# A four-layer image network in one kernel on one Trainium2 core: new products in its linear attention, and softmax transfers made for two steps at a time

## The chip, the cores and the metric

One NeuronCore of a Trainium2 chip runs the whole program in one launch. The metric is the device time in microseconds (us) from the start of the program to its end. The engines have short names in the profile: PE is the matrix unit (PEld its weight loads), DVE the vector unit, ACT the scalar unit, POOL and SP the two others, which here mostly issue DMA transfers. "SPq L2173" means an issue on SP's queue by line 2173 of the kernel.

## What is computed

The input is x of shape 2 x 512 x 32 x 32 in float32; write HW = 1024 for the positions of an image. Four layers follow one another: layer 0 is a deformable cross attention with a learned bias and an MLP; layer 1 a deformable convolution with a gate; layer 2 a linear attention; layer 3 a group norm and an attention of eight heads of 64 channels. Only the last two matter here:

```
# layer 2, per image, C = 512 channels, N = 1024 positions, d = 64
Qf, Kf = delu(wq x + bq)^T, delu(wk x + bk)        # delu(z) = 10 relu(z) + exp(10 min(z, 0))
V      = wv x + bv
KV     = Kf V^T                                    # d x C
norm   = 1 / (Qf (sum over n of Kf + 1e-10))
x      = x + gamma * (Qf KV * norm)^T

# layer 3, per image, 8 heads of 64 channels
h       = group_norm(x)
q, k, v = split(W_qkv h + b_qkv)
attn    = softmax(q k / 8)                         # 1024 x 1024 per head
out     = x + W_out (attn v) + b_out
```

## The kernel before

Layers 0 and 1 take the first 2940 us and are not touched. From there the program is a set of Python generators that are woven together: each `yield` is a place where the caller lets another generator issue some instructions. PE runs its instructions in the order in which they are issued, and so do the other engines and the DMA queues; in layer 3 that order is the written one (`manual_schedule`).

**Layer 2** is `Linear.run` (lines 1761 to 1902), once for each image. It runs for image 0 beside the gathers of layer 1's deformable convolution for image 1, and for image 1 beside the first matrix products of layer 3 (`att.queries_keys` and `att.values` of image 0); the tuple `BESIDE` says how many yields of `values` go behind each yield of `linear.run`. Its parts in order: two matmul groups for queries and keys with `delu` on them (an addition of the bias, then four passes: DVE, ACT, DVE, DVE); eight rounds that transpose 128 positions of x (`px`) and copy them out (`xt2`); in rounds 1 and 2 the transposed keys `kf`, held twice side by side; in round 3 the key sums `pks` (line 1827), eight matmuls of `kf` with a matrix of ones; from round 3 on the products `pkx` (line 1794): for each of the eight position blocks, four matmuls that have a 128 x 128 block of `xt2` as the stationary operand and move 64 columns of keys; then `kx`, a copy of `pkx`, and the product with `wv`.

**Layer 3** first makes queries, keys and values of image 0, then runs `heads`: 64 steps of 128 query positions for a pair of heads each (`first` are 32 steps of image 0, `second` 32 of image 1). A step is:

- `logits` (line 2133): four matmuls into two banks of 128 x 1024, one for each head of the pair. There are two such banks in all, so the logits of the next step start when the exponentials of this one have read them.
- for each of the two banks, the maximum (DVE, line 2236), the exponential with its sum (ACT, line 2242), written into a room `e2` of 8 KB in each partition, then a reciprocal and a scaling (`divide`, line 2254).
- `turn`: DVE transposes each half in 32 x 32 blocks (line 2166); after the second half, 16 DMAs of 64 KB move the blocks to where the transpose of the whole matrix needs them (line 2173), alternately on SP's and on POOL's queue, from the room into the tile `aT`, which holds two steps. Two `aT` tiles exist.
- `weigh` (line 2183): 16 matmuls of `v` with two steps' `aT`, issued in two halves, four steps after the first of the two; the copy of its output (line 2193) overwrites the queries of that step.

`room(at)` gives a step its room. Steps with `at % 3 < 2` take the two buffers of the tile `e3`; each third step borrows 8 KB from what is free then: the last two blocks of `q1` (the queries of image 1, written later), the value weights `w_v`, or the values `v[0]` of image 0. A room's next writer waits until its transfers have landed. `LENT` holds the steps at which the place changes. `w_out` is loaded over `w_v` at the steps in `LOADED`, on ACT's queue.

Within a step the order on the engines is set by this part of the loop, which makes the logits and exponentials of step `at + 1` before it turns step `at`:

```
if g == 1:
    e2, ahead = ahead[0], weights(at + 1) if at + 1 < len(work) else ((), ())
    turn(at, e2, 0)
    for part in ahead[1][:1]:
        self.divide(*part)
    turn(at, e2, 1)
```

Between these, PE gets work from `fill`: (steps, generator, yields) in turn: the values of image 1, its queries and keys, and the output projections of image 0 and of the first half of image 1 (`project`; its matmuls, like those of the values, go through `by_columns`, line 1962, as two halves of 64 columns). One yield of them is one 128 x 128 stationary block against 512 columns. After the last step come what is left of the weighings and of the projections (`last`), and then the last projection, whose stores go out on SP's queue.

Of the kernel before, what the change touches and what calls it, by code (L numbers as in the profile page):

```python
# [11 lines left out]
F32 = mybir.dt.float32  # L12
# [265 lines left out]
def layers(net, out):  # L278
# [12 lines left out]
    with ExitStack() as later:  # L291
# [106 lines left out]
        with ExitStack() as l1:  # L398
# [95 lines left out]
            with ExitStack() as ctx:  # L494
# [6 lines left out]
                for i, _ in enumerate(linear.run(1, bank, held)):  # L501
                    some(keys, 2)
                    some(values, BESIDE[i])
                    if i > 11:
                        next(terms)
# [19 lines left out]
BESIDE = (1, 2, 1, 1, 1, 1, 1, 1, 1, 1, 3, 3, 1, 1, 1, 1)  # L525
# [1213 lines left out]
def delu(nc, out, e, z):  # L1739

    nc.vector.tensor_scalar(e, z, 0.0, None, ALU.min)
    nc.scalar.activation(e, e, AF.Exp, scale=10.0)
    nc.vector.tensor_scalar(out, z, 0.0, 10.0, ALU.max, ALU.mult)
    nc.vector.tensor_tensor(out, out, e, ALU.add)


class Linear:
# [5 lines left out]
    def __init__(self, net, ctx, **kw):  # L1753
# [4 lines left out]
        self.ones = w.tile([128, 64], F32, name="ones2", tag="ones2")  # L1758
        nc.gpsimd.memset(self.ones, 1.0)
# [4 lines left out]
    def run(self, b, bank, kv_bank):  # L1764
# [5 lines left out]
        qk = []  # L1770
        for n in range(2):
# [11 lines left out]
            nc.vector.tensor_scalar(qf, pqk, net.vec("bqk", n), None, ALU.add)  # L1783
            delu(nc, qf, e, qf)
# [5 lines left out]
        kf = tmp.tile([128, 8, 2, 64], F32, name="kf", tag="kf")  # L1790

        def product(t, xt):
            for cc in range(CC):
                nc.tensor.matmul(
                    pkx[:, 64 * cc : 64 * cc + 64],
                    lhsT=xt[:, 128 * cc : 128 * cc + 128],
                    rhs=kf[:, t, 0, :],
                    start=(t == 0 and cc == 0),
                    stop=(t == 7 and cc == CC - 1),
                    skip_group_check=True,  # L1800
                )

        for t in range(8):
# [5 lines left out]
            xt = tmp.tile([128, C], F32, name="xt2", tag="xt2", bufs=4)  # L1809
# [4 lines left out]
            if t in (1, 2):  # L1814
                n = t - 1
                pk = bank("pk")
                for u in range(4):
                    at = slice(128 * u, 128 * u + 128)
                    nc.tensor.transpose(pk[:, at], qk[n][:, at], ident)
                keys = pk.rearrange("p (t v d) -> p t v d", v=2, d=64)[:, :, 1 - n : 2 - n, :]  # L1820
                nc.scalar.copy(
                    kf[:, 4 * n : 4 * n + 4, :, :], keys.to_broadcast([128, 4, 2, 64])
                )
            if t == 3:
                pks = bank("pks")
                for u in range(8):
                    nc.tensor.matmul(
                        pks[:, :64],
                        lhsT=kf[:, u, :, :].rearrange("p v d -> p (v d)"),
                        rhs=self.ones,  # L1830
                        start=(u == 0),
                        stop=(u == 7),
                    )
                ksum, norms = (
                    tmp.tile([128, 64], F32, name=name, tag=name) for name in ("ksum", "norms")
                )
                nc.vector.tensor_copy(ksum, pks[:, :64])
                nc.vector.tensor_scalar(norms, ksum, 1e-10, None, ALU.add)
# [22 lines left out]
            if t > 2:  # L1861
# [5 lines left out]
        for part in pending:  # L1867
            product(*part)
        kx = tmp.tile([128, CC, 2, 64], F32, name="kx", tag="kx")
        nc.scalar.copy(  # L1870
            kx,
            pkx[:, : 64 * CC]
            .rearrange("p (c d) -> p c d", d=64)
            .unsqueeze(2)
            .to_broadcast([128, CC, 2, 64]),
        )
        yield
# [77 lines left out]
LENT = 27, 37  # L1955
LOADED = 38, 39, 40, 41
# [14 lines left out]
class Attention:  # L1971
# [20 lines left out]
    def open_values(self, ctx, **kw):  # L1992
# [4 lines left out]
        self.q1 = self.late.tile([128, CC, HW], F32, name="qk1", tag="qk1")  # L1997
        self.small = net.pool(ctx, "l3_small", 2, **kw)
        self.w_v = self.load_qkv(self.w_pool, 2)
        self.b_v = net.load_row("b_v_row", self.w_pool)  # L2000

    def load_out(self, k):

        if k == 0:
            self.w_out = self.w_pool.tile([128, CC, C], F32, name="w_out_t", tag="w_qkv2")
# [319 lines left out]
```

## Time and profile before

| what | value |
|---|---|
| times of three runs | 3664.64, 3664.69, 3670.85 us; median 3664.69 |
| the profiled execution | 3666.18 us; its span from first to last instruction 3664.2 us |
| granted PE clock, mean | 0.995 of full |
| PE busy in the span | 98% |
| 2940 to 3030 us (layer 2 of image 0 beside gathers) | PE busy 90.0 of 90.0 us, DVE 55.2, ACT 26.2 |
| 3178 to 3246 (layer 2 of image 1) | PE 68.0 of 68.0, DVE 27.2, ACT 9.6 |
| 3250.4 to 3631 (the 64 steps of layer 3) | PE 369.2 of 380.6, DVE 312.0, ACT 309.1, POOL 242.5; DMA share 0.66, 181 GB/s |
| 3631 to 3664.2 (after the last step) | PE 28.0 of 33.2 |

The profiled execution is one more run of the same program with the hardware's recorder on; all lines quoted below are from it. Rows of the windows view give the window, its length, then busy us and count for PE, PEld, DVE, ACT and POOL, then the granted PE clock, the mean busy share of the 16 DMA engines and their GB/s. Rows of the timeline give the start, the duration (of the whole group, where "x8" stands behind it), the engine, the line and the operation, and in brackets the idle time before it and what ended it; "SPq" rows are the issues of that queue. Rows of the waits view give who waited for what: us in total, times, longest. Rows of the chain, followed back from the last instruction, read like the timeline. A float32 matmul is two records of PE.

### The profile page before, as it was taken

To read this page: it belongs to the slowest core of one execution; us is meant where nothing else is said; L and a number is where in the kernel's file an instruction comes from. 1 tells how busy PE (TensorE), PEld (TensorE's weight loads), DVE (VectorE), ACT (ScalarE), POOL (GpSimd) and SP (SyncE) were. 2 spreads that over 40 slices of the span, in tenths; PEclk is the share of its full clock that TensorE was granted. 3 is DMA by queue.
4 is the path that set the end of the run, shared out by engine and by line. 5 is a ranking of instruction groups with operands and counts; after the bars stand their busy time and mean duration, and the time that the engine had idled before them with its cause. 6 is when DMAs were issued, how large, how long until landed. Compare 5 with 4: busy or idle time off the path is not lost.

```text
span 3664.2 us, 60466 instructions
## 1 busy us (share of the span) xinstructions
PE 3604.2 (98%) x24684; PEld 1402.5 (38%) x24684; DVE 2768.8 (76%) x3192; ACT 2591.6 (71%) x2885; POOL 417.3 (11%) x693
## 2 busy tenths in 40 slices
PE   7999999999999999999999999999999999999999
PEld 4333333333333333333333444444444454444444
DVE  6999999999999999999999821051048657268786
ACT  6999999999999999999999821131113324348875
POOL 0000000000000000000000000000025125026665
PEclk9999999999999999999999999999999999999999
DMA  3000000000000000000001010002246547126675
GB/s 117 1 24 24 17 9 24 24 1 24 24 24 1 24 24 24 1 24 24 1 24 58 16 49 0 0 26 79 70 137 227 179 162 274 37 70 184 174 197 171
DMA packets 96071, 235.80 MB, mean 64 GB/s; under 512 B 21252, under 2 KB 26884, under 8 KB 93108
## 3 DMA queue, kind: packets, MB, share of 16 engines
q0 software_dynamic: 38080, 112.47, 10.0%
q1 hardware_dynamic: 55844, 115.26, 9.7%
q10 hardware_dynamic: 1872, 4.22, 0.4%
q8 instruction: 195, 3.19, 0.4%
q14 instruction: 80, 0.66, 0.1%
HBM read 156.11 MB, written 8.65 MB: 45 GB/s over the span
## 4 chain that ended last, share of the span: by engine, by line
PE 73%; ACT 15%; DVE 5%; issue 3%; DMA 3%; POOL 1%; SPq 0%; DVEq 0%; ACTq 0%; POOLq 0%
PE ph L925 33%; PE ph L1186 6%; PE acc L1175 6%; ACT h L915 5%; PE sim L944 5%; PE po L1680 4%; ACT hi L1014 4%; ACT lo L1011 4%; PE pw L1544 3%; PE pl L2133 2%; PE po L2183 2%; PE pq L1968 2%; PE po L1126 2%; PE pq L1962 1%; DMA got<-table,idx 1%
## 5 line engine op out<-in xcount | busy, mean ns | idle before, releaser
L925 PE MATMUL ph<-h,w_t 128*32 128x512 f32 x16384 | 1796.8, 593 | 7.1 <-ACT h L915 3.9
L900 DVE TENSOR_TENSOR h<-ab 128x1024 f32<-128x1024 f32 x1024 | 1205.3, 1218 | 45.9 <-PE ph L925 44.0
L925 PEld LDWEIGHTS ph<-h,w_t 128*32 128x32 f32 x16384 | 565.2, 110 | 1203.5 <-issue 1067.0
L915 ACT ACTIVATE h<-h 128x1024 f32<-128x1024 f32 x832 | 925.2, 1112 | 8.6 <-DVE size L874 7.8
L937 DVE SCALAR_TENSOR_TENSOR hi<-lo,low_w,hi 128x1024 f32<-128x1024 f32 x512 | 654.3, 1278 | 20.1 <-ACT hi L1014 19.8
L1014 ACT ACTIVATE hi<-ph,size_b,size 128x1024 f32<-128x1024 f32 x512 | 644.1, 1258 | 21.6 <-PE ph L925 21.6
L1011 ACT ACTIVATE lo<-ph,vec_t 128x1024 f32<-128x1024 f32 x512 | 595.4, 1163 | 44.0 <-PE ph L925 39.0
L1680 PE MATMUL po<-fold,turned 128*128 128x512 f32 x576 | 261.7, 597 | 0.4 <-issue 0.4
L1194 ACT ACTIVATE h<-ph,vec_t 128x512 f32<-128x512 f32 x64 | 44.0, 687 | 303.1 <-PE ph L1186 303.0
L944 PE MATMUL sim<-hi,w 128*32 128x512 f32 x2048 | 249.4, 592 | 0.0
L1262 POOL MEMSET pad<- 128x136 f32 x2 | 0.4, 220 | 2061.1 <-PE ph L925 2061.1
L1186 PE MATMUL ph<-xn,room 128*128 128x512 f32 x512 | 230.8, 594 | 0.0
L1175 PE MATMUL acc<-h,mlp_w_t 128*128 128x512 f32 x512 | 229.8, 592 | 0.0
L1589 POOL DMA_INDIRECT got<-table,idx x144 | 156.7, 1088 | 538.2 <-DVE sum L1613 273.9
L1613 DVE SCALAR_TENSOR_TENSOR sum<-got,wts,sum 128x256 f32<-128x256 f32 x432 | 182.3, 478 | 40.3 <-ACT sum L1609 32.5
L2236 DVE TENSOR_REDUCE m<-pl 128x1 f32<-128x1024 f32 x128 | 150.7, 1219 | 61.1 <-PE pl L2133 60.5
L2173 POOL DMA_DIRECT2D aT<-e x344 | 168.2, 497 | 199.8 <-DVE s L2253 111.8
L1680 PEld LDWEIGHTS po<-fold,turned 128*128 128x128 f32 x576 | 105.0, 192 | 107.0 <-issue 106.4
L1642 ACT COPY turned<-pt 128x512 f32<-128x512 f32 x72 | 41.9, 582 | 146.9 <-PE pt L1636 136.4
L1175 PEld LDWEIGHTS acc<-h,mlp_w_t 128*128 128x128 f32 x512 | 97.3, 190 | 122.4 <-issue 121.7
L1186 PEld LDWEIGHTS ph<-xn,room 128*128 128x128 f32 x512 | 96.6, 191 | 117.0 <-issue 116.4
L1611 DVE TENSOR_SCALAR sum<-got,wts 128x256 f32<-128x256 f32 x38 | 12.4, 352 | 165.9 <-PE pt L1636 152.1
(274 smaller groups left out, 2980.5 us busy)
## 6 DMA issues: line engine op xcount, KB each, us to landing
ab<-feat_d SPq DMA_DIRECT2D x64, 512.0 KB, 4.6
aT<-e SPq DMA_DIRECT2D x344, 64.0 KB, 2.6
aT<-e POOLq DMA_DIRECT2D x344, 64.0 KB
room<-in_dc_w_dram SPq DMA_DIRECT2D x9, 1024.0 KB, 4.8
dc_w_t<-in_dc_w_dram SPq DMA_DIRECT2D x10, 512.0 KB, 4.1
aT<-qk SPq DMA_DIRECT2D x72, 64.0 KB, 2.7
aT<-qk POOLq DMA_DIRECT2D x72, 64.0 KB
aT<-v SPq DMA_DIRECT2D x72, 64.0 KB, 2.7
```

The source lines that it names most:

```text
L900: nc.vector.tensor_tensor(h1.rearrange("p (y x) -> p y x", x=32), at_x[:, k : k + 1, :].to_broadcast([128, 32, 32]), at_y[:, k, :].unsquee ...
L915: nc.scalar.activation(h1, h1, AF.Relu)
L925: nc.tensor.matmul(ph[32 * t : 32 * t + 32, half(n)], lhsT=w2[:, c0 : c0 + 32], rhs=pair[t // 2][:, half(n)], start=True, stop=True, skip_ ...
L937: nc.vector.scalar_tensor_tensor(hi, lo, low_w, hi, ALU.mult, ALU.add)
L944: nc.tensor.matmul(sim[32 * t : 32 * t + 32, half(n)], lhsT=w3[:, 30 - j : 62 - j], rhs=sums[t][:, half(n)], start=(j == 0), stop=(j == 30 ...
L1011: nc.scalar.activation(lo, phs[0], AF.Relu, bias=b2_lo)
L1014: nc.scalar.activation(hi, phs[1], AF.Relu, bias=size_b, scale=size)
L1175: nc.tensor.matmul(accs[oc], lhsT=self.w2[:, m, 128 * oc : 128 * oc + 128], rhs=hs[m], start=(m == 0), stop=(m == 15),)
L1186: nc.tensor.matmul(ph, lhsT=self.w1[:, k, 128 * m : 128 * m + 128], rhs=xn[:, k, :], start=(k == 0), stop=(k == CC - 1),)
L1613: nc.vector.scalar_tensor_tensor(t[:, q, :], g[:, s, :], w, t[:, q, :], ALU.mult, ALU.add)
L1680: nc.tensor.matmul(self.out, lhsT=turned[:, at : at + 128], rhs=self.folded.w[k][:, i, :], start=(k == 0 and i == 0), stop=(k == 8 and i = ...
L2173: (nc.sync, nc.gpsimd)[i % 2].dma_start(out=turned[at // 2][32 * u : 32 * u + 32, at % 2, a, :, :], in_=e2[32 * a : 32 * a + 32, u, :, :],)
```

## The change

In layer 2, `delu` takes its argument already multiplied by ten (the multiplication joins the addition of the bias) and so has one pass less; its last pass also gives the totals over positions. The key sums become one matmul of two columns of totals with a matrix that adds the two halves (`fold`). The products hold the keys stationary (64 columns) and move 512 columns of `xt2`; even and odd position blocks go to the two halves of the output's partitions, so a copy to `parts`, four transposes and two DVE passes follow, which put the result into the old layout of `kx`. One more yield stands in between, and `BESIDE` has one more entry.

In layer 3, `PAIRS` names for each pair of steps the place of its exponentials: `a` a tile of 16 KB in each partition, `q` and `w` parts of one new tile `shared` that holds `q1` (four blocks) and `w_v` (two blocks), `v` the values of image 0. A pair's transfers are issued together after its odd step: 16 DMAs of 128 KB, each for both steps, where there were 32 of 64 KB. The four pairs with a dot (steps 28 to 35) have single rooms and single transfers as before, by `SINGLE`. `w_out` is loaded one step earlier. Four yields of the values of image 1 (`lead`) go between the first exponentials and their scaling, and `fill` is shifted to match. After the last step, what is left of the projections goes ahead of the two last weighings, where it stood between them.

```diff
--- before
+++ after
@@ -503,3 +503,3 @@
                     some(values, BESIDE[i])
-                    if i > 11:
+                    if i > 12:
                         next(terms)
@@ -524,3 +524,3 @@
-BESIDE = (1, 2, 1, 1, 1, 1, 1, 1, 1, 1, 3, 3, 1, 1, 1, 1)
+BESIDE = (1, 2, 1, 1, 1, 1, 1, 1, 1, 1, 2, 2, 2, 1, 1, 1, 1)
@@ -1738,8 +1738,7 @@
-def delu(nc, out, e, z):
+def delu(nc, out, e, z, total):
     nc.vector.tensor_scalar(e, z, 0.0, None, ALU.min)
-    nc.scalar.activation(e, e, AF.Exp, scale=10.0)
-    nc.vector.tensor_scalar(out, z, 0.0, 10.0, ALU.max, ALU.mult)
-    nc.vector.tensor_tensor(out, out, e, ALU.add)
+    nc.scalar.activation(e, e, AF.Exp)
+    nc.vector.scalar_tensor_tensor(out, z, 0.0, e, ALU.max, ALU.add, accum_out=total)
@@ -1757,4 +1756,6 @@
         self.bv = net.load_row("bv_row", w)
-        self.ones = w.tile([128, 64], F32, name="ones2", tag="ones2")
-        nc.gpsimd.memset(self.ones, 1.0)
+        self.fold = w.tile([128, 2, 64], F32, name="halves", tag="halves")
+        ident = net.cst("ident")
+        for v in range(2):
+            nc.vector.tensor_tensor(self.fold[:, v, :], ident[:, :64], ident[:, 64:], ALU.add)
@@ -1770,2 +1771,3 @@
         qk = []
+        totals = tmp.tile([128, 4], F32, name="totals", tag="totals")
         for n in range(2):
@@ -1782,4 +1784,8 @@
             e = tmp.tile([128, 512], F32, name="e2", tag="e2")
-            nc.vector.tensor_scalar(qf, pqk, net.vec("bqk", n), None, ALU.add)
-            delu(nc, qf, e, qf)
+            nc.vector.tensor_scalar(qf, pqk, net.vec("bqk", n), 10.0, ALU.add, ALU.mult)
+            delu(nc, qf, e, qf, totals[:, n : n + 1])
+            rows = slice(64 * (1 - n), 128 - 64 * n)
+            nc.vector.tensor_copy(
+                totals[rows, 2:4], totals[rows, n : n + 1].to_broadcast([64, 2])
+            )
             qk.append(qf)
@@ -1789,14 +1795,14 @@
-        kf = tmp.tile([128, 8, 2, 64], F32, name="kf", tag="kf")
+        kf = tmp.tile([128, 8, 64], F32, name="kf", tag="kf")
         def product(t, xt):
-            for cc in range(CC):
-                nc.tensor.matmul(
-                    pkx[:, 64 * cc : 64 * cc + 64],
-                    lhsT=xt[:, 128 * cc : 128 * cc + 128],
-                    rhs=kf[:, t, 0, :],
-                    start=(t == 0 and cc == 0),
-                    stop=(t == 7 and cc == CC - 1),
-                    skip_group_check=True,
-                )
+            r = 64 * (t % 2)
+            nc.tensor.matmul(
+                pkx[r : r + 64, :],
+                lhsT=kf[:, t, :],
+                rhs=xt,
+                start=(t < 2),
+                stop=(t > 5),
+                skip_group_check=True,
+            )
@@ -1808,3 +1814,3 @@
                 )
-            xt = tmp.tile([128, C], F32, name="xt2", tag="xt2", bufs=4)
+            xt = tmp.tile([128, C], F32, name="xt2", tag="xt2", bufs=5)
             if t % 2 == 0:
@@ -1819,21 +1825,19 @@
                     nc.tensor.transpose(pk[:, at], qk[n][:, at], ident)
-                keys = pk.rearrange("p (t v d) -> p t v d", v=2, d=64)[:, :, 1 - n : 2 - n, :]
-                nc.scalar.copy(
-                    kf[:, 4 * n : 4 * n + 4, :, :], keys.to_broadcast([128, 4, 2, 64])
-                )
+                keys = pk.rearrange("p (t v d) -> p t v d", v=2, d=64)[:, :, 1 - n, :]
+                nc.scalar.copy(kf[:, 4 * n : 4 * n + 4, :], keys)
             if t == 3:
                 pks = bank("pks")
-                for u in range(8):
-                    nc.tensor.matmul(
-                        pks[:, :64],
-                        lhsT=kf[:, u, :, :].rearrange("p v d -> p (v d)"),
-                        rhs=self.ones,
-                        start=(u == 0),
-                        stop=(u == 7),
-                    )
-                ksum, norms = (
-                    tmp.tile([128, 64], F32, name=name, tag=name) for name in ("ksum", "norms")
+                nc.tensor.matmul(
+                    pks[:, :2],
+                    lhsT=self.fold.rearrange("p v d -> p (v d)"),
+                    rhs=totals[:, 2:4],
+                    start=True,
+                    stop=True,
+                )
+                ksum = tmp.tile([128, 2], F32, name="ksum", tag="ksum")
+                norms = tmp.tile([128, 64], F32, name="norms", tag="norms")
+                nc.vector.tensor_copy(ksum, pks[:, :2])
+                nc.vector.tensor_scalar(
+                    norms, ksum[:, 0:1].to_broadcast([128, 64]), 1e-10, None, ALU.add
                 )
-                nc.vector.tensor_copy(ksum, pks[:, :64])
-                nc.vector.tensor_scalar(norms, ksum, 1e-10, None, ALU.add)
                 pkx = kv_bank("pkx")
@@ -1860,3 +1864,3 @@
                     )
-            if t > 2:
+            if t == 4:
                 for part in pending:
@@ -1868,10 +1872,16 @@
             product(*part)
+        parts = tmp.tile([128, 512], F32, name="kx_parts", tag="e2")
+        nc.scalar.copy(parts, pkx)
+        yield
+        pkt = bank("pkt")
+        for cc in range(CC):
+            at = slice(128 * cc, 128 * cc + 128)
+            nc.tensor.transpose(pkt[:, at], parts[:, at], ident)
         kx = tmp.tile([128, CC, 2, 64], F32, name="kx", tag="kx")
-        nc.scalar.copy(
-            kx,
-            pkx[:, : 64 * CC]
-            .rearrange("p (c d) -> p c d", d=64)
-            .unsqueeze(2)
-            .to_broadcast([128, CC, 2, 64]),
+        even, odd = (
+            pkt.rearrange("p (c v d) -> p c v d", v=2, d=64)[:, :, v : v + 1, :] for v in range(2)
         )
+        shape = [128, CC, 2, 64]
+        nc.vector.tensor_copy(kx, even.to_broadcast(shape))
+        nc.vector.tensor_tensor(kx, kx, odd.to_broadcast(shape), ALU.add)
         yield
@@ -1954,4 +1964,5 @@
-LENT = 27, 37
-LOADED = 38, 39, 40, 41
+PAIRS = "aq" * 3 + "awawawaw" + "...." + "va" * 7
+SINGLE = "01201201"
+LOADED = 37, 38, 39, 40
@@ -1996,5 +2007,7 @@
         self.late = net.pool(ctx, "l3_late", 1, **kw)
-        self.q1 = self.late.tile([128, CC, HW], F32, name="qk1", tag="qk1")
+        self.shared = self.late.tile([128, 6, HW], F32, name="qk1", tag="qk1")
+        self.q1 = self.shared[:, :CC, :]
         self.small = net.pool(ctx, "l3_small", 2, **kw)
-        self.w_v = self.load_qkv(self.w_pool, 2)
+        self.w_v = self.shared[:, CC:, :].rearrange("p a (k m) -> p (a k) m", m=C)
+        net.nc.sync.dma_start(out=self.w_v, in_=net.ins["w_qkv"][:, 2, :, :])
         self.b_v = net.load_row("b_v_row", self.w_pool)
@@ -2003,4 +2016,3 @@
-        if k == 0:
-            self.w_out = self.w_pool.tile([128, CC, C], F32, name="w_out_t", tag="w_qkv2")
+        self.w_out = self.w_v
         self.net.nc.scalar.dma_start(out=self.w_out[:, k, :], in_=self.net.ins["w_out"][:, k, :])
@@ -2118,2 +2130,3 @@
         self.tmp = net.pool(ctx, "l3_tmp", 2)
+        self.pair = self.tmp.tile([128, 2, 2 * HW], F32, name="e3", tag="e3", bufs=1)
         self.ps_l = net.psum(ctx, "l3_logits", 2)
@@ -2122,3 +2135,3 @@
-    def heads(self, work, fill, last):
+    def heads(self, work, lead, fill, last):
@@ -2143,11 +2156,19 @@
-            if at % 3 < 2:
-                return self.tmp.tile([128, 4, 2, 256], F32, name="e3", tag="e3")
-            if at < LENT[0]:
-                place = self.q1[:, 2:4, :].rearrange("p c i -> p (c i)")
-            elif at < LENT[1]:
-                place = self.w_v.rearrange("p k m -> p (k m)")
+            home = PAIRS[at // 2]
+            if home == ".":
+                k = int(SINGLE[at - 28])
+                place = self.w_v.rearrange("p k m -> p (k m)") if k == 2 else self.pair[:, k, :]
+                return place.rearrange("p (u r i) -> p u r i", u=4, r=2)
+            return pair(at // 2)[:, at % 2, :, :, :]
+
+        def pair(k):
+            home = PAIRS[k]
+            if home == "a":
+                place = self.pair
+            elif home == "v":
+                place = self.v[0].rearrange("p (s t) m -> p s (t m)", s=2)
             else:
-                place = self.v[0][:, 0:4, :].rearrange("p t m -> p (t m)")
-            return place.rearrange("p (u r i) -> p u r i", u=4, r=2)
+                c = "q.w".index(home)
+                place = self.shared[:, c : c + 4, :].rearrange("p (s c) i -> p s (c i)", s=2)
+            return place.rearrange("p s (u r i) -> p s u r i", u=4, r=2)
@@ -2170,7 +2191,12 @@
                 turned[at // 2] = self.tmp.tile([128, 2, 4, 2, 256], F32, name="aT", tag="aT")
+            both = PAIRS[at // 2] != "."
+            if both and at % 2 == 0:
+                return
+            aT = turned[at // 2]
             for i in range(16):
                 a, u = i % 4, (i % 4 + i // 4) % 4
+                to, source = slice(32 * u, 32 * u + 32), slice(32 * a, 32 * a + 32)
                 (nc.sync, nc.gpsimd)[i % 2].dma_start(
-                    out=turned[at // 2][32 * u : 32 * u + 32, at % 2, a, :, :],
-                    in_=e2[32 * a : 32 * a + 32, u, :, :],
+                    out=aT[to, :, a, :, :] if both else aT[to, at % 2, a, :, :],
+                    in_=pair(at // 2)[source, :, u, :, :] if both else e2[source, u, :, :],
                 )
@@ -2199,2 +2225,3 @@
         ahead = weights(0)
+        some(*lead)
         for part in ahead[1]:
@@ -2229,3 +2256,3 @@
                 weighing.pop(0)
-        for _ in chain(weighing[0], last, weighing[1]):
+        for _ in chain(last, *weighing):
             pass
@@ -2279,6 +2306,6 @@
     fill = [
-        (1, islice(vals, 2), 2),
-        (3, islice(vals, 12), 12),
-        (11, vals, 18),
-        (7, att.queries_keys(1, 0, spare), 16),
+        (1, islice(vals, 1), 1),
+        (3, islice(vals, 11), 11),
+        (10, vals, 16),
+        (8, att.queries_keys(1, 0, spare), 16),
         (7, att.queries_keys(1, 1, spare), 16),
@@ -2295,3 +2322,3 @@
             pass
-        att.heads(first + second, fill, chain(halved, output(1, 512, 256)))
+        att.heads(first + second, (vals, 4), fill, chain(halved, output(1, 512, 256)))
     for _ in att.project(1, 768, 256, out, att.last_bank):
```

## The prediction, made before the change was run

> **What bounds the kernel now.** The page first, then stage windows, then the timeline of one step of layer 3, then the chain of waits.
>
> ```profile
> PE 3604.2 (98%) x24684; PEld 1402.5 (38%) x24684; DVE 2768.8 (76%) x3192; ACT 2591.6 (71%) x2885; POOL 417.3 (11%) x693
> ```
>
> The change touches nothing before 2940 us. The windows split the rest (us, busy time of each engine, granted clock, DMA share, GB/s):
>
> ```profile
> 3178.00:3246.00 68.00, 68.00 (x256) 35.75 (x255) 27.20 (x51) 9.62 (x16) 0.00 (x0) 1.00 0.00 0
> 3250.40:3337.40 87.00, 82.49 (x416) 34.49 (x416) 73.14 (x96) 70.80 (x97) 51.09 (x105) 0.98 0.58 157
> 3337.40:3468.30 130.90, 129.70 (x739) 57.19 (x740) 104.81 (x133) 111.30 (x156) 86.20 (x177) 1.00 0.65 178
> 3468.30:3626.50 158.20, 152.52 (x836) 66.45 (x836) 129.51 (x165) 123.85 (x174) 101.74 (x210) 0.99 0.70 194
> ```
>
> Layer 2 of image 1 (first row) is pure PE: PE work saved there is time saved. The other rows are the 64 steps of layer 3 (15, 22 and 26 step distances: 5.80, 5.95, 6.08 us a step). PE is nearly full, but DVE and ACT at 80 to 85% and a DMA share of 0.6 to 0.7 leave little slack; all four close a loop, which one step shows:
>
> ```profile
> 3359.89 4.96 SPq L2173 DMA_DIRECT2D aT<-qk  x8
> 3360.36 3.91 POOL L2173 DMA_DIRECT2D aT<-qk  x8 [2.45 <-ACT e L2254]
> 3360.64 2.35 DVE L2236 TENSOR_REDUCE m<-pl 128x1 f32<-128x1024 f32 x2 [0.78 <-PE pl L2133]
> ...
> 3361.90 1.11 ACT L2242 ACTIVATE e<-pl,m 128x1024 f32<-128x1024 f32 x1 [0.85 <-DVE m L2236]
> ...
> 3363.03 1.11 ACT L2242 ACTIVATE e<-pl,m 128x1024 f32<-128x1024 f32 x1
> ...
> 3364.11 1.22 DVE L2166 STREAM_TRANSPOSE e<-e 128x1024 f32<-128x1024 f32 x1
> 3364.28 1.99 PE L2133 MATMUL pl<-qk 64*128 64x512 f32 x8
> ```
>
> A step's first exponential starts at 3361.90; the second transpose of the step before it, which releases that step's 16 transfers, ends at 3364.11 + 1.22 = 3365.33, 3.43 later. SP needs 4.96 for its eight issues, POOL 3.91, nearly the whole 5.85 us step. The last SP issue begins about 4.5 after the transpose and lands 2.4 later (the DMA view's median is 2.6): about 6.9 in all. Three rooms mean that a room is wanted again two steps after its transfers start, less 3.43: 2 x 5.85 - 3.43 = 8.3. So 6.9 fits with 1.4 to spare, and only disturbed steps wait:
>
> ```profile
> ACT e L2242 <- DMA aT<-v: 10.7, 5, 3.4
> ACT v L2242 <- DMA aT<-e: 8.7, 4, 3.1
> ```
>
> **The change, layer 3 pairs.** Where `PAIRS` has a letter (28 of 32 pairs; steps 28 to 35 go singly, as before), the transfers of two steps are issued together after the odd step's transpose: 16 of 128 KB in place of 32 of 64 KB. Issues on SP and POOL halve, if one costs by the instruction (saving 4.96 and 3.91 a pair on queues that are not the end); if by the row, eight on SP take 9.9 and the last lands at about 11.2, which the range takes in. Bytes and 2 KB rows stay: 2.1 MB, now in one burst. There are two pair rooms, so the pair after next wants the room again after the same 2T - 3.43 = 8.3, but twice the bytes must land in it. A second waiter has the same date: `weigh` of that pair stands on PE's queue just after the same step's logits.
>
> What does 2.1 MB cost? No row shows such a burst, so bounds. From below: 6.9, as now, if only the issues set the pace. From above: today's megabyte moves from 3372.1 to 3377.2:
>
> ```profile
> 3372.10:3377.20 5.10, 5.10 (x33) 2.49 (x31) 4.53 (x5) 3.97 (x7) 3.34 (x7) 1.00 0.74 206
> 3482.50:3485.50 3.00, 3.00 (x18) 1.07 (x14) 2.44 (x5) 2.96 (x6) 1.32 (x3) 1.00 1.06 268
> ```
>
> At 206 GB/s two take 10.2, with the 1.9 of start and landing (6.9 - 5.0) 12.1. The first row's DMA engines are busy 0.74; the second, where the w_out loads pile up on the transfers, shows them full, and full is 268 GB/s. That row is nearest to a burst: 2.1 / 0.268 = 7.8, plus 1.9, plus 0.3 because POOL's first packets come half a microsecond after SP's: 10.0. I take 10.0.
>
> The first exponential is then 10.0 - 8.3 = 1.7 late. The exponential behind it, the next logits (whose bank it frees) and PE follow. Some is absorbed: where logits start early on the first half (2.85 us long at 3289.16) the next maximum comes 4.83 after the last (3286.38 to 3291.21), not 5.51, so 0.7 is slack. Loss 1.0 a pair. The pairs that wait on a pair are 2 to 13 and 20 to 31: 24. **+24 us** (0 at a landing of 9.0; +74 at 12.1).
>
> [...]
>
> The 2.7 to 2.9 us pauses that POOL makes between issues (chain, at 3320, 3500 and 3591) would hide inside a DMA-bound burst; I credit them to the gain side of the range only, up to 7.
>
> **Layer 3, start.** PE idles here for the first exponentials, and the next logits run slow in a stretch whose granted clock is 0.81:
>
> ```profile
> 3254.22 4.41 PE L2133 MATMUL pl<-qk 64*128 64x512 f32 x8 [4.01 <-ACT e L2242]
> ```
>
> `lead` puts four yields of values there (4 x 0.86 = 3.44). The second exponential still ends near 3255.2; normal logits then end 1.5 earlier. **-1.5** (0 to -3.4).
>
> **Tail.** The chain's end:
>
> ```profile
> 3633.19 5.36 PE po L2183 x32
> 3638.55 12.06 PE pf L1962 x88
> 3650.61 3.45 PE po L2183 x32
> 3654.06 6.92 PE pf L1962 x64
> ```
>
> PE is free at 3631.2 but waits for transfers, and the first `po` takes 5.36 for the 3.45 of the second. Now `last` (12.06) goes first, needs no pending transfer, and ends at 3643.3; both weighings follow, the last pair having landed by 3634.2 + 10.0 = 3644.2 against a need at 3646.7. PE ends at 3657.1, not 3661.0. **-3.9** (0 if the banks of `last` wait on DVE).
>
> **Layer 2.** Per image, as the chain shows it (a float32 matmul is two records):
>
> ```profile
> 3194.04 1.73 PE pks L1827 x16
> 3195.78 2.68 PE pkx L1794 x24
> ```
>
> Key sums: 8 matmuls, 1.73; products: 24 records 2.68, the other 40 in five groups of 0.84 to 1.03; 6.8 together. New: one two-column matmul (0.1 to 0.3), eight of 64 columns by 512 in alternating halves, which overlap as `pv L1962` does (0.43 each, 3.44; 6.9 if not), four transposes like `px` (0.86). 8.5 becomes 4.6: -4.0 for image 1 (-0.7 if not overlapped). `delu` loses one of four DVE passes and `kx` gains two; DVE has 40 of 68 us free, and two yields (1.72) stand between each new link of parts, transposes, sums; without that cover each image loses up to 2.2. Image 0: PE is busy 60 of 60 from 2940, but from 3038 to 3080 the chain is gathers (11.53 of `got` at 3047), so I take -2.5 (0 to -4.0). The extra yield moves the w_q and w_k loads one deform pass later, far ahead of use. **-6.5.**
>
> **Sum.** +24 - 1.5 - 3.9 - 6.5 = +12. The profiled execution took 3666.18 (span 3664.2), 1.5 over the median of 3664.69; so 3678 by the profile, 3677 as a median: +0.3%.
>
> **Rivals.**
> - *The burst fits, faster.* Place: the first exponential of each even step; condition: a pair lands within 9.0 (then 2.1 MB in 9.0 - 1.9 - 0.3 = 6.8 us, about 310 GB/s where the row has 268). For: rows at full share vary, twice the row count per issue gives fewer semaphore writes, and issue is 4.96 of 5.85 now. Against: the 268 GB/s row. Price: -1.5 - 3.9 - 6.5, and 4 of the POOL pauses: 3649. Chance 0.27.
> - *It cancels.* Landing 9.5: 0.5 x 24 = 12 against -12: 3665. Chance 0.13.
> - *Column halves don't overlap in layer 2* (each has its own moving tile). Then layer 2 gives 1 and the burst decides: 3682. Against: `po L2183`, with two moving tiles, runs 16 records in 1.73. Chance 0.05.
>
> Forecast 0.55. About 0.2% (7 us) is what can be told from no change here. The slower cases hold 0.60, the cancelling one 0.13, the faster 0.27. The range: from 3649, the faster case, to a landing of 11 (+48): 3702.
>
> **What would show it.** Right: the DMA view in 2 us slices shows bursts at share 1.0 and then nothing; SP's eight issues a pair last about 5; waits of ACT `e L2269` on DMA grow to 24 long ones of 1 to 2 us; pairs of steps take 12.7. The layer 2 stage of image 1 shrinks by 4 and the tail's chain shows `pf` before `po`. Wrong: pairs landing below 9 and ACT's waits on DMA gone; or stalls that are not on transfers.

## The result: slower by 0.8%

The changed kernel takes 3697.34 us (median of four runs, 3695.54 to 3700.53) against 3666.11 for the kernel before on the same chip: a ratio of 1.0082 with a 95% interval of 1.0066 to 1.0098. Its profiled execution has a span of 3693.6 us, 29.4 more than that of before. Forecast were +12 us and slower, with a range up to 3702.

Where the 29.4 us lie can be read from the starts of the steps' first maxima in the two traces (step 0 at 3250.39 before and 3243.53 after; step 2 at 3263.31 and 3254.47; step 63 at 3626.51 and 3660.02):

| stretch | forecast | measured in the trace |
|---|---|---|
| up to the first matmul of layer 2 (nothing changed there) | 0 | -1.1 |
| layer 2, image 0 | -2.5 | -1.7 |
| layer 2, image 1 | -4.0 | -4.1 |
| step 0 to step 2 (early yields) | -1.5 | -2.0 |
| step 2 to step 63 (pairs) | +24 | +42.4 |
| step 63 to the end (order of the tail) | -3.9 | -4.1 |
| sum | +12 | +29.4 |

Of the forecast's terms, all but one came out within 1 us; the first row, where nothing was changed, shows that two executions can differ by 1.1 without it. The page of after: PE's work is as before, POOL has a quarter less to do, and a transfer on SP's queue lands in the median 4.1 to 5.0 after its issue, for which 2.6 to 2.7 stood before.

```profile
PE 3602.7 (98%) x24568; PEld 1388.6 (38%) x24568; DVE 2773.6 (75%) x3204; ACT 2587.4 (70%) x2885; POOL 313.9 (8%) x467
...
aT<-e SPq DMA_DIRECT2D x112, 128.0 KB, 4.1
...
aT<-qk SPq DMA_DIRECT2D x56, 128.0 KB, 5.0
```

Chain of waits of after, one burst (start, duration, what): the pair of steps 12 and 13, whose second transpose ends at 3337.93.

```profile
3341.82 1.73 SPq L2199
...
3343.60 1.36 SPq L2199
...
3345.00 2.81 DMA aT<-e
...
3347.96 1.95 PE po L2209 x16
```

The last transfer lands at 3347.81, 9.9 after the transpose. Of most pairs the trace tells the landing of only 3 or 4 of the 16 transfers; the latest of these has a median of 9.84 over the 28 pairs, so that for whole pairs the median is 9.84 or more. What stands behind it on the chain is PE itself, in the weighing.

The windows of the burst of steps 10 and 11 show the DMA engines full while it lasts, and empty after it:

```profile
3327.60:3330.60 3.00, 3.00 (x24) 1.35 (x20) 2.19 (x2) 0.94 (x1) 1.78 (x4) 1.00 1.00 285
3330.60:3333.60 3.00, 3.00 (x12) 0.97 (x8) 2.91 (x6) 2.96 (x6) 0.00 (x0) 1.00 0.95 289
3333.60:3336.60 3.00, 3.00 (x19) 1.21 (x19) 3.00 (x3) 2.98 (x5) 0.00 (x0) 1.00 0.03 8
```

The waits of after in layer 3 (us in total, times, longest), PE's:

```profile
PE po L2209 <- DMA aT<-e: 12.4, 10, 2.5
PE po L2209 <- DMA aT<-v: 11.6, 4, 5.9
PE po L2209 <- DMA out_dram<-x_all: 9.2, 5, 2.9
PE po L2209 <- DMA aT<-qk: 7.8, 5, 2.1
```

and the two longest of ACT's for a transfer:

```profile
ACT e L2269 <- DMA aT<-e: 20.6, 9, 3.7
...
ACT v L2269 <- DMA aT<-v: 11.8, 3, 6.3
```

The four rows of PE add up to 41.0 us ahead of the weighing. (Who ended a wait is inferred by the profile. A weighing reads only `aT` and `v`, so the row that names the stores to `out_dram` is counted with the others.) Before the change it was 7.1:

```profile
PE po L2183 <- DMA aT<-v: 3.6, 2, 2.9
PE po L2183 <- DMA aT<-e: 2.3, 2, 2.0
PE po L2183 <- DMA aT<-qk: 1.2, 1, 1.2
```

So two engines wait for the same transfers: ACT for the room, PE for the data.

### The profile page after: what moved, and what is told of

Read it like the earlier page. It is cut to its first block, busy times and chain, and to the rows that moved or that the text cites. A ratio compares the mean times of both kernels' runs of the same rounds, so it can differ in the third digit from the quotient of the medians.

```text
span 3693.6 us, 59317 instructions
## 1 busy us (share of the span) xinstructions
PE 3602.7 (98%) x24568; PEld 1388.6 (38%) x24568; DVE 2773.6 (75%) x3204; ACT 2587.4 (70%) x2885; POOL 313.9 (8%) x467
## 2 busy tenths in 40 slices
DMA packets 88896, 235.72 MB, mean 64 GB/s; under 512 B 14084, under 2 KB 19716, under 8 KB 85940
## 3 DMA queue, kind: packets, MB, share of 16 engines
q1 hardware_dynamic: 52260, 115.25, 9.8%
## 4 chain that ended last, share of the span: by engine, by line
PE 63%; ACT 14%; issue 9%; DVE 4%; DMA 4%; SPq 3%; POOL 1%; ACTq 0%; POOLq 0%; DVEq 0%
PE ph L925 33%; ACT h L915 5%; PE sim L944 4%; PE ph L1186 4%; PE acc L1175 4%; ACT hi L1014 4%; ACT lo L1011 4%; PE po L1680 3%; SPq L2199 3%; DMA got<-table,idx 2%; PE pq L1979 2%; PE po L1126 1%; PE pl L2146 1%; PE po L2209 1%; PE pw L1544 1%
## 5 line engine op out<-in xcount | busy, mean ns | idle before, releaser
L2209 PE MATMUL po<-aT,v 128*64 128x256 f32 x1024 | 129.5, 397 | 41.3 <-DMA aT<-e 12.4
```

The lines of the kernel that those rows point to most:

```text
L2209: nc.tensor.matmul(po[64 * r : 64 * r + 64, :].rearrange("p (a q) -> p a q", q=32), lhsT=self.v[b][:, t, c0 : c0 + 64], rhs=aT[:, :, :, r, ...
```

## Experiments

The theory at the outset, called the burst theory: a pair's 2.1 MB fills the DMA engines and lands 10 us after the transpose, where 8.3 are free. Its rivals were that the issues on SP's queue set the pace, that the rooms or the other parts of the change are at fault, and, on the side of those who wait, that only ACT's room or only PE's weighing matters. The length of steps 2 to 28 (13 pairs) and 44 to 62 (9 pairs), from maximum to maximum, is given beside the times, each from the one profiled execution of its run; before the change they took 150.1 and 107.9, after it 171.2 and 118.9.

**Single transfers in the new rooms.**

```diff
-            both = PAIRS[at // 2] != "."
+            both = False
```

> All of the change stays, its rooms for two steps too, but the transfers are issued singly: 16 of 64 KB after every step. Burst theory (a pair's 2.1 MB fills the DMA engines and lands 10 us after the transpose, where 8.3 are free): a step's megabyte lands in about 6.9 again, ACT waits for no room (four rooms give 14 us), PE stands before the weighing some 7 us in all as before instead of 41, so the 42 us that the 64 steps lost come back: 3697 - 42 = 3655, 3650 to 3658. Rival, the rooms (the loss comes from where the exponentials now lie, or from the other parts of the change): stays at 3685 or more.

Measured: 3646.44 us, ratio to the kernel before 0.9947 (0.9932 to 0.9962); steps 2 to 28 take 149.3, 44 to 62 take 105.9. The rooms and the rest of the change are cleared: the grouping of the transfers alone takes the time. It fell below the expected range, since the fourth room also does away with waits that the kernel before had. This version beats both kernels.

**The three other parts with the rooms and transfers of before.**

```diff
-            home = PAIRS[at // 2]
...
+            if at % 3 < 2:
+                place = self.pair[:, at % 3, :]
+            elif at < 27: ...            # q1, w_v, v[0] as before the change
-            both = PAIRS[at // 2] != "."
+            both = False
```

> Layer 2, the four early yields and the order after the last step as in the change; rooms and transfers of layer 3 as before the change (three single rooms, 16 transfers of 64 KB a step). Burst theory: the time before less the three other parts as the trace of after has them (1.7 + 4.1 in layer 2, 2.0 at the start, 4.1 at the end): 3666 - 12 = 3654. Beside the run with four rooms it tells what a fourth room is worth: 0 if the transfers are early enough, up to 10 if the waits of ACT on DMA (29 us in the trace of before) reach PE. If one of the three parts gave nothing by itself, it stays nearer to 3660.

Measured: 3652.46 us, 0.9962 (0.9949 to 0.9976), as the sum of the terms says. Steps 2 to 28 take 150.2, as before the change. The fourth room, with which `w_out` is also loaded one step earlier, is worth 5.9 by the two spans (3650.6 and 3644.7): 0.8 in steps 2 to 28, 2.4 in 36 to 44 and 1.5 in 44 to 62.

**Fewer issues on SP.**

```diff
-                (nc.sync, nc.gpsimd)[i % 2].dma_start(
+                (nc.gpsimd, nc.sync)[both and i % 3 == 0 or not both and i % 2 == 0].dma_start(
```

> The change with a pair's 16 transfers dealt 6 to SP and 10 to POOL, in place of 8 and 8. Burst theory: the bytes and the engines are the same, so a pair still lands some 10 us after the transpose and the time stays at 3697 within 5. Queue theory (SP's eight issues, which take 7.5 us where eight of half the size took 5.0, set the landing): SP is done after 5.6, POOL after 0.7 + 5.3, both land by 8.5, the waits shrink to a tenth and the time falls to 3660 to 3670.

Measured: 3702.89 us, 1.0098 (1.0082 to 1.0114). This is 0.9 beyond the 5 us that were allowed, on the side away from the queue theory. Six issues on SP took 6 us where eight had taken 7.5, that is, 1.0 each in place of 0.94; single ones of 64 KB take 0.62. In the trace of after, where POOL paused for 2.87 within the pair of steps 20 and 21, SP's eight issues of 128 KB took 5.08, or 0.63 each, for 7.5 where POOL did not pause: there they were slow while the other queue's transfers were under way, and did not set the pace themselves. The queue theory falls.

**Fill ahead of the weighing.** The whole step's share of `fill` goes to PE before the first half of the weighing in even steps.

```diff
-                if at % 2 == 0 and at >= 4 and g in (0, 2):
-                    some(weighing[0], 1)
-                if fill:
+                early = at % 2 == 0 and at >= 4
+                for _ in range((4 if g == 0 else 0) if early else 1):
...
+                if at % 2 == 0 and at >= 4 and g in (0, 2):
+                    some(weighing[0], 1)
```

> The change with all fill of an even step (values, queries and keys, projections; about 2.3 yields of 0.86 us) put on PE ahead of the first half of the weighing, not spread over the step. Theory of the weighing (PE's idle time stands before the weighing, 41 us of it, because nothing else is queued ahead): about 1.5 us more work lies ahead in each of 24 pairs, most of the idle time is covered, 3697 - 25 to 30 = 3667 to 3672. Theory of the exponential (what ends last is the late room on ACT, and the weighing only shares its date): the next logits come no earlier and the time stays within 6 of 3697.

Measured: 3695.88 us, 1.0079 (1.0065 to 1.0093). PE's idle time ahead of the weighing falls from 41.3 to 17.5, and yet nothing is won. Steps 2 to 28 take 169.7; steps 28 to 36, which have no pairs, take 53.0 in place of 50.5, some 0.6 more for two steps. So this order has a price of its own, and it lies in the logits. Windows of the logits' tile `pl` alone (PE's time for them is the first number behind the length), steps 2 to 28 and 28 to 36, first of after, then of this run:

```profile
3254.47:3425.67 171.20, 58.33 (x210) 22.90 (x208) 61.26 (x53) 60.31 (x104) 0.97 0.59 159
3425.67:3476.19 50.52, 16.22 (x64) 6.84 (x64) 18.84 (x16) 18.62 (x32) 1.00 0.64 173
```

```profile
3252.53:3422.22 169.69, 68.38 (x210) 26.37 (x208) 61.24 (x52) 60.29 (x104) 1.00 0.58 157
3422.22:3475.23 53.01, 20.08 (x65) 7.18 (x64) 18.85 (x17) 18.61 (x32) 1.00 0.63 174
```

The logits take 1.0 us more for two steps without pairs and 0.8 more with pairs. The price is thus about what was won at the weighing, and the run by itself does not decide between the two theories.

**Half the bytes.**

```diff
-                    out=aT[to, :, a, :, :] if both else aT[to, at % 2, a, :, :],
-                    in_=pair(at // 2)[source, :, u, :, :] if both else e2[source, u, :, :],
+                    out=aT[to, 1, a, :, :] if both else aT[to, at % 2, a, :, :],
+                    in_=pair(at // 2)[source, 1, u, :, :] if both else e2[source, u, :, :],
```

> The change with the even step's half of every paired transfer left out (its weights stay zero in what is weighed): 16 transfers of 64 KB a pair, issued at the same place after the odd step. Burst theory: 1 MB in a burst lands some 6.9 after the transpose as before the change, nothing waits for it, the time is that of the run with four rooms: 3646, 3642 to 3652. Rival, the late issue (what costs is that nothing is sent until the odd step is done, whatever its size): 3685 or more.

Measured: 3701.93 us, 1.0095 (1.0078 to 1.0112), which by the time alone would speak for the late issue. The steps say otherwise. Windows of steps 2 to 28 of this run, of the changed kernel and of the kernel before:

```profile
3260.67:3410.86 150.19, 148.99 (x816) 64.64 (x816) 127.31 (x164) 127.85 (x176) 51.00 (x104) 1.00 0.34 92
```

```profile
3254.47:3425.67 171.20, 156.01 (x816) 67.33 (x816) 128.50 (x164) 125.58 (x176) 54.76 (x104) 0.97 0.59 159
```

```profile
3263.31:3413.41 150.10, 149.41 (x823) 64.80 (x824) 127.90 (x164) 126.38 (x176) 101.42 (x208) 1.00 0.67 182
```

This run and the next leave out the weights of the even steps of a pair, so they do not compute the whole layer, and only their times are of use. With half the bytes in as many transfers, issued at the same late place, the pairs land after 7.0, and PE waits for them only 1.2 us in all up to 3400. The time went into steps 28 to 36, 102.4 in place of 50.5: two fixed tiles had taken the place of the rotating `aT`, and a single transfer of an even step then stood ahead of the second half of the weighing that reads the same tile. A second run mends that:

```diff
-                    some(weighing[0], 1)
+                    some(weighing[0], 2 if 28 <= at < 38 and g == 0 else 1)
```

> As the run with half the bytes (the even step's half of every paired transfer is left out), with both halves of the weighing issued together in steps 28 to 36, so that the single transfers of those steps no longer stand ahead of a weighing that reads the same tile. Burst theory: steps 28 to 36 take 50 again, not 102, and the rest stays as it was without waits: 3702 - 52 = 3650, 3643 to 3653. Late-issue rival: 3685 or more.

Measured: 3655.87 us, 0.9962 (0.9949 to 0.9976), 3 above the expected range. Steps 2 to 28 take 149.9 and 44 to 62 102.8; what is too much lies ahead of step 0, which begins at 3250.16 in place of 3243.01 with four rooms: the zeroing of the two tiles runs there. So the late issue by itself costs nothing that these steps show; it is the bytes.

**Rows of 4 KB.**

```diff
-            return place.rearrange("p s (u r i) -> p s u r i", u=4, r=2)
+            return place.rearrange("p (u s r i) -> p u s r i", u=4, s=2, r=2)
-... tile([128, 2, 4, 2, 256], F32, name="aT", tag="aT")
+... tile([128, 4, 2, 2, 256], F32, name="aT", tag="aT")
```

> The change with a pair's two steps side by side in the room and in aT, so that a transfer moves rows of 4 KB in place of 2 KB, half as many, in the same 16 transfers of 128 KB; the copy behind the weighing puts the queries back in order. If the bytes fill the DMA engines (285 GB/s at share 1.0 in the trace of after), the landing stays near 10 and the time within 6 of 3697. If it is the rows (each has a fixed part), a pair lands earlier, by 8.3 if a 4 KB row takes 1.6 times as long as one of 2 KB, and the time falls to 3655 to 3670.

Measured: 3705.92 us, 1.0102 (1.0085 to 1.0119). The packets on SP's side fell from 52260 to 45092, and most pairs still landed after 9.5 to 10.9; steps 2 to 28 took 175.5. That is 4.3 over the change's 171.2, and the time is 2.6 beyond the 6 that were allowed. Both can be put down to something else, one wait of PE:

```profile
PE pv L1973 <- ACT qk L2284: 6.4, 1, 6.4
```

In this layout the exponentials of step 14 already lie over half of the value weights (place `w`), and PE's last two value products of image 1 come behind them, one of which then no longer reads weights (the run with the old start and tail, below, shows the same). The landing does not come earlier in any case, so fewer rows buy nothing: with the same bytes in half the rows steps 2 to 28 take 175.5 for 171.2, with half the bytes they take 149.9.

**A third place for pairs in the second half**, without and with the fill ahead of the weighing.

```diff
-PAIRS = "aq" * 3 + "awawawaw" + "...." + "va" * 7
+PAIRS = "aq" * 3 + "awawawaw" + "...." + "va" + "vha" * 4
...
+            elif home == "h":
+                place = self.h[1].rearrange("p (s c) i -> p s (c i)", s=2)
```

> The change with a third place for pairs from step 42 on, the normalized image 1 (h), which is read no more from there: order v a v, then h a v in turn. ACT's wait for a room is gone in steps 44 to 63; PE's wait of the weighing for the same transfers stays. These steps took 13 us more in the trace of after than with four rooms. Theory of the exponential (the room alone decides): 10 to 13 of it come back, 3684 to 3687. Theory of the weighing: nothing comes back, 3697. Theory of the same date (each wait holds the step by itself): nothing or up to 4 comes back here, and covering both is needed.

Measured: 3693.69 us, 1.0074 (1.0057 to 1.0090), 3.6 less than the change by the medians, with intervals that overlap. In the trace steps 44 to 62 take 119.9, but that execution took 3699.53, and its granted clock is 0.96 in these steps where it was 1.00 in after, which is worth an estimated 5 us (0.04 x 119.9). ACT waits for no transfer there any more, and PE still waits. Its waits in these steps:

```profile
PE po L2211 <- DMA out_dram<-x_all: 5.9, 3, 2.5
PE po L2211 <- DMA aT<-h: 2.4, 1, 2.4
PE po L2211 <- DMA aT<-v: 2.2, 1, 2.2
PE po L2211 <- DMA aT<-e: 1.8, 1, 1.8
```

> The third place for pairs and the fill ahead of the weighing together, so that from step 44 on neither ACT nor PE stands against the landing. Theory of the same date: steps 44 to 62 take 110 or less (118.9 in after, 118.2 to 118.9 with the fill ahead alone), 3696 - 9 = 3687 or less. Theory of the exponential: as the third place alone, 3684 to 3687. If it stays at 3694 or more, neither wait is what holds these steps and something else late (the odd steps without fill, the transfers into aT) does.

Measured: 3687.79 us, 1.0060 (1.0043 to 1.0077); steps 44 to 62 take 114.0. Removing ACT's wait alone gave up to 4 of the 13 us and not the 10 to 13 that the theory of the exponential asks for. With the fill ahead of the weighing in both runs, and the mean granted clock at 0.997 in both, the third place is worth 6 (120.1 to 114.0; 8 by the medians, 3695.88 to 3687.79), which the theory of the weighing alone does not allow. So both waits hold the steps, and each hides a part of the other; that they have exactly the same date is not shown. The 114.0 missed the expected 110. Of the 8 us that are left to the 105.9 with four rooms, some 5 (nine pairs at 0.6) are the price of this order of the fill as steps 28 to 36 showed it, and the last 3 are not accounted for.

**Layer 2 alone**, on the kernel before (the new `Linear`, `delu`, `BESIDE`).

> The kernel before with the change's layer 2 alone. By the two traces 1.7 for image 0 and 4.1 for image 1: 3666 - 6 = 3660; the forecast had 6.5. If the column halves did not overlap on PE it would be within 2 of the time before.

Measured: 3661.01 us against 3668.69, 0.9977 (0.9968 to 0.9986). Both the forecast's 6.5 and the 5.8 of the traces lie within this.

**Four rooms with the old start and tail.**

```diff
-            some(*lead)
-        for _ in chain(last, *weighing):
+        for _ in chain(weighing[0], last, weighing[1]):
...
-        (1, islice(vals, 1), 1), (3, islice(vals, 11), 11), (10, vals, 16), (8, att.queries_keys(1, 0, spare), 16),
+        (1, islice(vals, 2), 2), (3, islice(vals, 12), 12), (11, vals, 18), (7, att.queries_keys(1, 0, spare), 16),
```

> The run with four rooms without the four early yields and with the old order after the last step. By the traces the early yields are worth 2.0 (the time from step 0 to step 2) and the order 4.1 (from step 63 to the end): 3646.4 + 6 = 3652.5. If the early yields only moved work, 3650.5; if the order depended on the paired transfers, the end takes what it took before the change, 37.7 from the maximum of step 63, or less.

Measured: 3666.82 us, 0.9993 (0.9984 to 1.0002): 19 more than with four rooms by the two spans (3663.7 and 3644.7), not 6. Step 63 to the end takes 38.9 in place of 33.5, so the order is worth 5.4 here; steps 0 to 2 take 13.7 in place of 10.9. Another 8.2 lie in steps 2 to 28: 5.7 are one wait of PE, and behind it PE is slower for a while (the next 16 matmuls of the weighing take 3.63, the 16 after those 1.90):

```profile
PE pv L1973 <- ACT qk L2280: 5.7, 1, 5.7
```

The last two of the 32 value products of image 1 now come behind the exponentials of step 15, which lie over their weights (place `w`); they wait for these, and, by the order of the program, what they multiply is no longer the weights, so that this version computes something else in a part of image 1. So the shift of `fill` by the early yields is also what makes the new rooms possible, and this run prices more than the two ends.

**The pairs alone**, with the layer 2, start and tail of before.

> The kernel before with the paired rooms and transfers alone: layer 2, the start and the order after the last step as before. Burst theory: the loss of 42 in the 64 steps by itself, 3666 + 42 = 3708, 3702 to 3712. The forecast's term was 24: 3690. If the parts work against each other it lies away from both.

Measured: 3718.07 us, 1.0130 (1.0114 to 1.0145), 49 more than before. Steps 2 to 28 take 176.1: the same collision costs 4.9 over the 171.2 of the change (PE waits 5.6 for ACT once). The rest, 44, is the loss of 42 of the change and little more, now without the parts that paid for it. The forecast's 24 is excluded.

## Why the prediction was right in its sign, and short in its size

- *The loop and its date.* Right: a megabyte lands after 6.9 to 7.0 (7.0 is the median of the 64 steps before the change) and is free, two land after 9.84 or more where 10.0 was forecast. The rate from the full-engine row (268 GB/s) was near: the burst above ran at 285 to 289. The issuing was not what set the landing: two issues moved from SP to POOL won nothing (1.0098 for 1.0082).
- *Who pays.* The step that failed is "0.7 is slack", and with it the loss of 1.0 a pair. It was read from one step whose logits took 2.85, where those of its neighbours take 1.99 to 2.13. PE has no such slack on the average: it is busy 149.4 of 150.1 us in steps 2 to 28 before the change, though that time also holds logits drawn out like those 2.85. From step 2 to step 63 PE's idle time rose by 33.7 (7.6 to 41.3), 1.4 for each of 24 pairs. The forecast named the second waiter, the weighing, but counted only the first exponential. Measured are 42.4 / 24 = 1.8 a pair. The forecast's own 1.7 without the slack would give 41; that this is so near is in part luck, since the 42.4 hold a share of the clock, for which there was no term.
- *What was left out.* The other 8.6 of the 42.4 are busy time: the same matmuls became slower (mean of `po` 397 ns for 389; 156.0 busy in steps 2 to 28 for 149.4, at a mean granted clock of 0.97). No term stood for the clock; the estimate in the section on the hardware puts some 6.8 of the 8.6 down to it. Nor was there one for the `w_out` loads, which now fall into a burst: the pair of steps 36 and 37, whose second transpose ends at 3492.91, landed at 3506.33, after 13.4, and PE waited 5.9 for it, the longest wait of all. The chain of after shows that landing:

```profile
3500.21 6.12 DMA aT<-v
```

- *Start, tail, layer 2.* Right within 1 us each. The tail's new order in the chain of after, `last` ahead of both weighings, each now without a wait:

```profile
3662.72 13.77 PE pf L1973 x96
3676.49 6.91 PE po L2209 x64
3683.40 6.93 PE pf L1973 x64
```

- In layer 2 the eight products stand on the chain in two groups of four, and the column halves overlap as was assumed (0.47 a matmul for the 0.43 forecast), which rules out the rival on that:

```profile
3194.49 1.87 PE pkx L1800 x8
...
3209.37 1.87 PE pkx L1800 x8
```

- *The rivals.* "The burst fits" needed 310 GB/s; the burst of steps 10 and 11 reached 285 to 289, the next one 275 to 302 in slices of 2 us. The fewer semaphore writes that it named agree with the pages (14084 packets under 512 B for 21252, 16 less for each of the 448 transfers saved), and the pairs landed late all the same. "It cancels" needed a landing of 9.5; at least 20 of the 28 pairs landed later than that. POOL's pauses, credited to the gain side, came at steps 21 and 43, and no gain from them shows.

## What to carry to other kernels

Putting transfers together halved the number of issues, and that was worth nothing here, where the issues did not set the pace; what it costs is that the first half's bytes wait for the second half, so that a link at a mean share of 0.67 becomes one that is full for 6 us (1.00 and 0.95 in the windows above) and then all but idle (0.03). Where buffers are short, send each part when it is ready: with single transfers, and the rooms and all else of this change, the kernel gains 0.5%. And where the bound engine has no idle time, take no slack from one quiet place for the lateness of its inputs: count all of it, for every engine that waits for the same date, and, as here, the slower clock behind some of the long waits as well (0.50 for 3.41 us).

## What the hardware showed that was not expected

Behind some of PE's waits its granted clock was at half. After a wait of 1.87 us at 3293.60 it was 0.50 for 3.41 us; after one of 2.52 us at 3547.51 it stayed at 1.00. Windows of after, the wait and what follows:

```profile
3293.60:3295.47 1.87, 0.00 (x1) 0.03 (x1) 1.87 (x3) 0.03 (x1) 0.00 (x0) 1.00 0.48 121
3295.47:3297.00 1.53, 1.53 (x10) 1.11 (x12) 0.98 (x3) 1.53 (x3) 0.00 (x0) 0.61 0.02 5
3297.00:3298.50 1.50, 1.50 (x10) 0.78 (x6) 1.02 (x2) 1.50 (x3) 0.00 (x0) 0.50 0.00 0
...
3547.51:3550.03 2.52, 0.00 (x0) 0.03 (x1) 1.52 (x2) 0.12 (x1) 0.00 (x0) 1.00 0.37 126
3550.03:3552.00 1.97, 1.97 (x17) 1.33 (x17) 0.85 (x2) 1.97 (x3) 0.00 (x0) 1.00 0.00 0
```

Half the clock came with five of the waits in the 64 steps (1.87, 2.12, 2.47, 2.91 and 5.86 us), and not with others of up to 2.5 us. In the clock records of after the five stretches begin at 3295.80, 3323.11, 3387.96, 3504.01 and 3654.20; each lasts 3.41 us, but the one from 3504.01 lasts 6.83, the first 3.1 of which PE still waited. So the length of a wait alone does not tell which one slows the work behind it, and what does is not shown. In the first stretch 16 matmuls of `po` take 3.4 us (595 ns each in the mean), where the 16 behind the burst of steps 12 and 13 take 1.95. As an estimate, 3.4 us at 0.50 cost about 1.7 of work each. The kernel before has one such stretch in the same steps, from 3599.37:

```profile
3599.37:3602.78 3.41, 3.36 (x16) 1.71 (x16) 1.35 (x3) 3.33 (x6) 1.17 (x3) 0.50 0.65 185
```

By this estimate four more of them account for 4 x 1.7 = 6.8 of the 8.6 of extra busy time; the other 1.8 stay open.

The second surprise is in the second run with half the bytes: while POOL zeroed two tiles, DVE's small copy beside it, of 4 elements for each partition, took 3.17 us; in the trace of after, which zeroes no tiles there, the same copy took 0.17. Why it took so long is not shown. Timeline of the run with half the bytes:

```profile
3232.62 6.96 POOL L2136 MEMSET aT<- 128x4096 f32 x2 [76.37 <-PE pa L1904]
...
3236.44 3.17 DVE L1936 COPY mean<-st 128x4 f32<-128x4 f32 x1
```
